# A post-norm transformer block: rotation and gating in PSUM, row maxima in pairs, a third bank for products

## The chip, the cores and the metric

The kernel runs on one core of a Trainium2 chip. A core has five engines that matter here: TensorE (matrix products; PE in the profile, PEld its weight loads), VectorE (DVE), ScalarE (ACT), GpSimd (POOL) and SyncE (SP), which here only issues transfers. They run beside each other; each works through its own instructions in order and waits on semaphores for the others. Matrix products land in PSUM, a small memory of eight banks, each holding 512 float32 numbers in each of 128 partitions. Operands and results otherwise lie in SBUF. The metric is the device time of one execution in microseconds; times are medians of several runs.

## What is computed

```python
def attn(x, Wq, bq, Wk, bk, Wv, bv, Wo, bo):        # 16 query heads of 32, one key/value head
    q = (x @ Wq + bq).reshape(B, T, H, HD).transpose(0, 2, 1, 3)
    k, v = (x @ Wk + bk)[:, None], (x @ Wv + bv)[:, None]
    q, k = rotary(q), rotary(k)      # [x1*cos - x2*sin, x2*cos + x1*sin] of the two halves of a head
    attn = softmax(q @ k^T / sqrt(HD))
    return (attn @ v).transpose(0, 2, 1, 3).reshape(B, T, D) @ Wo + bo

def ffn(x, w1, w2, w3):              # weights are made ternary: clip(round(w / mean|w|), -1, 1)
    return bitlinear(sigmoid(bitlinear(x, w1)) * bitlinear(x, w2), w3)

x = layernorm(x + attn(x, ...))
x = layernorm(x + ffn(x, ...))
```

B = 4 batches, T = 512 rows, D = 512, F = 1408 hidden columns; all float32.

## The kernel before

One core does all four batches in one program. Everything is laid out with features on the partitions: 512 features are NC = 4 chunks of 128 (a chunk is four heads), 512 rows are NT = 4 tiles of 128, the 1408 hidden columns are NF = 11 tiles.

**Order.** The program's order on every engine is written by hand: each helper (`act`, `dve`, `pool`, `mm`, `move`) pins its instruction to the place in which it is emitted, so the Python code from line 679 is the schedule. It walks 64 *steps*, one for each batch b, chunk c and tile t. A step emits, in this order: `scores` of this tile (lines 375 to 410: transposed scores of four heads into two double banks of `ps_sc`, minus the row maxima, then exponentials `es` on ScalarE); `weigh` of the step before (line 416, the product with v, into `acc`); row maxima for the step LEAD = 7 ahead (`find_maxima`, line 705); and *fill*. Fill is other work in pieces of about 1.8 us: projections of later batches (`project_in`, line 237), the output projection (`project_out`, line 517) and the feed-forward (`feed_forward`, line 551). `fill.draw(us)` (line 661) emits pieces until the drawn time is used up, with `least` at least one; the time that a step draws is `pace`, 1.8, 3.8, 4.8 and 4.6 us for the four batches. Work with a delay stands in the list `late`; `due()` (line 689), called twice in a step, counts a slot and advances what has come due: the spreading of maxima, `normalize`, loads of x, layer norms, stores of q.

**Two kinds of step.** Up to step PER + 4 = 20, maxima are found in pairs of tiles, both before the fill, and `quantize` (2 or 3 jobs a step, three in each of the seven lead steps) emits the ternary weights: an absolute sum over each raw weight tile, or a sign on ScalarE and a `scalar_tensor_tensor` on VectorE (tile `raw`), with loads and stores on POOL's queue. From step 20 on the maxima come as one tile, two tiles, one tile, with fill between them. A single one goes into the bank with the tag `den`, a pair into a double bank of `ps_sc` (line 348).

**Banks.** `ps_sc` has two double banks, `ps_acc` one bank `acc` and one bank `den`, `ps_mm` two banks `mm` for all other products.

**Rotation.** `turn` (line 225) is a generator in two halves. A projection lands in a bank; ScalarE copies it with its bias into SBUF (`r` or `kv`); the first half on VectorE makes a = (product + bias) * cos from PSUM, which together with the copy frees the bank. After the next piece of fill the second half swaps the halves of each head (`stream_shuffle` of the copy into `w`), multiplies `w` by the signed sine table in SBUF and adds a and w.

**Gating.** `feed_forward` makes tanh of the gate product on ScalarE (`th`), then hw = (th + 1) * up from PSUM into SBUF on VectorE, which frees the bank, and `split` (line 506) cuts hw into a rounded head (ScalarE) and a tail (VectorE) for two exact single-pass products.

**POOL.** From the second batch on POOL adds up the exponentials (`total`, four additions in a step), and normalizes: `normalize` (line 432) copies the row sums to SBUF, sends them through DRAM into a compact tile `few`, takes the reciprocal on VectorE, sends it back and spreads it (`rden`), and multiplies on POOL, one `due` turn for each stage. `load_x` (line 494) loads the four tiles of x and adds bo on POOL, all four in one turn.

Of the kernel before, what the change touches and what calls it, by code (L numbers as in the profile page):

```python
# [27 lines left out]
def postln_block(  # L28
# [74 lines left out]
    wo_sb = const.tile([P, NC, D], F32, name="wo_sb")  # L103
    bq_sb = const.tile([P, NC], F32, name="bq_sb")
    bkv_sb = const.tile([P, 1], F32, name="bkv_sb")
    bo_sb = const.tile([P, D], F32, name="bo_sb")
# [50 lines left out]
    def quantized():  # L157
# [38 lines left out]
        for k, (m, last, f) in enumerate(jobs):  # L196
# [18 lines left out]
            yield  # L215


    swap = [(i + HALF) % HD for i in range(HD)]
# [5 lines left out]

    def turn(outs, src, bias, r, n):

        w = work.tile([P, T], F32, tag="rot_b", name="w")
        a = work.tile([P, T], F32, tag="rot_c", name="a", bufs=1)
        dve.scalar_tensor_tensor(a[0:n], src[0:n], bias[0:n], cos_sb[0:n], ALU.add, ALU.mult)
        yield  # L230
        dve.stream_shuffle(w[0:n], r[0:n], swap)
        dve.tensor_tensor(w[0:n], w[0:n], sin_sb[0:n], ALU.mult)
        for out, rows in outs:
            dve.tensor_tensor(out, a[rows], w[rows], ALU.add)
        yield

    def project_in(b):

        s = batches[b]
        n = P - HD  # L240
        while now < NC * NT * (b - 2):
            yield 0

        pk = ps_mm.tile([P, T], F32, tag="mm", name="pk")
# [4 lines left out]
        kv = work.tile([P, T], F32, tag="rot_a", name="kv")  # L249
        act.activation(kv, pk, AF.Identity, bias=bkv_sb)  # L250
        s.kT = work.tile([P, T], F32, tag="kT", name="kT", bufs=3)
        rotation = turn(
            [(s.kT[0:n], slice(0, n)), (s.kT[n:P], slice(0, HD))], pk, bkv_sb, kv, n
        )
        next(rotation)
        yield 1.8
        next(rotation)
        if b > 0:
            late.append((slot + 2, split_k(b)))
        for c in range(NC):  # L260

            while b + 1 == B and c + 2 >= NC and not batches[0].projected:
                yield 0
            pq = ps_mm.tile([P, T], F32, tag="mm", name="pq")
            for d in range(NC):
                mm(pq, wq_sb[c][:, d, :], s.xT[d], d == 0, d == NC - 1)
                if d == 1:
                    yield -1.8
            r = work.tile([P, T], F32, tag="rot_a", name="r")
            act.activation(r, pq, AF.Identity, bias=bq_sb[:, c : c + 1])  # L270
            if b == 0:

                if c == 0:
                    room = work.tile([P, NC, T], F32, tag="y0", name="room", bufs=1)
                q = s.q[c] = room[:, c, :]
            else:
                q = work.tile([P, T], F32, tag="q", name="q")
            rotation = turn([(q, slice(0, P))], pq, bq_sb[:, c : c + 1], r, P)
            next(rotation)
            if c == 0:  # L280
                pv = ps_mm.tile([P, NT, HD], F32, tag="mm", name="pv")
# [4 lines left out]
            yield 1.8  # L286
            next(rotation)
            if b > 0:
                late.append((slot + 2, store_q(b, c, q)))
            s.done = c + 1  # L290
        load_xT(NC if b == 0 else 2)

# [49 lines left out]
    def maximum(b, c, i, chunks, q):  # L342


        s = batches[b]
        if i == 0 and chunks[0] == 0:
            s.mx[c] = small.tile([P, NG, NT], F32, tag="mx", name="mx")
        if len(chunks) == 1:
            ps = ps_acc.tile([P, 1, T], F32, tag="den", name="pmax")
        else:  # L350
            ps = ps_sc.tile([P, 2, T], F32, tag="sc", name="pmax")
        for n, t in enumerate(chunks):
            mm(ps[:, n, :], q[:, ts(t, P)], s.kr, True, True)
        dve.tensor_reduce(s.mx[c][:, i, chunks[0] : chunks[-1] + 1], ps, AX.X, ALU.max)

    def spread(b, c):


        s = batches[b]
        pm = ps_mm.tile([NG * NT, P], F32, tag="mm", name="pm")  # L360
# [12 lines left out]
        yield  # L373
# [58 lines left out]
    def normalize(b, c):  # L432

        s = batches[b]
        if b > 0:
            s.den = ps_acc.tile([P, T], F32, tag="den", name="den")
            columns(s.den, ones[:, 0:HD], s.total, True, True)

        sums = work.tile([P, T], F32, tag="sums", name="sums", bufs=1)
        act.copy(sums, s.den)  # L440
        yield
        flat = [dram.tile([NG, T], F32, tag=f"flat{i}", name="flat", bufs=3) for i in range(2)]
        move(flat[0], sums.rearrange("(i r) k -> i r k", r=HD)[:, 0])
        yield
        few = small.tile([P, NG * T // P], F32, tag="few", name="few")
        move(few, flat[0].rearrange("i (r j) -> (i r) j", r=HD))
        yield
        dve.reciprocal(few, few)
        move(flat[1].rearrange("i (r j) -> (i r) j", r=HD), few)
        yield  # L450
        rden = work.tile([P, T], F32, tag="rden", name="rden", bufs=1)
        for i in range(NG):
            move(rden[ts(i, HD), :], flat[1][i].partition_broadcast(HD))
        yield
        pool.tensor_tensor(s.ctxT[c], s.ctxT[c], rden, ALU.mult)
        yield
# [37 lines left out]
    def load_x(b):  # L494
        batches[b].x = []
        for t in range(NT):
            xt = xp.tile([P, D], F32, tag="x", name="xt")
            move(xt, x[b, ts(t, P), :])
            batches[b].x.append(xt)
        yield  # L500
        for xt in batches[b].x:
            pool.tensor_tensor(xt, xt, bo_sb, ALU.add)
        yield

# [12 lines left out]
    def project_out(b):  # L517
# [4 lines left out]
        for t in range(NT):  # L522
            po = ps_mm.tile([P, D], F32, tag="mm", name="po")
            for c in range(NC):
# [16 lines left out]
        for t in range(NT):  # L541
            pt = ps_mm.tile([P, NC, P], F32, tag="mm", name="pt")
            for c in range(NC):
# [7 lines left out]
    def feed_forward(b):  # L551
# [8 lines left out]
        def product(k, m):  # L560
# [3 lines left out]
            if len(w3[k]) < len(parts[k]):  # L564
                w3[k].append(load_weight(2, parts[k][len(w3[k])]))
            g = ps_mm.tile([P, T], F32, tag="mm", name="gu")
            for c in range(NC):
# [13 lines left out]
        for k, fs in enumerate(parts):  # L581
            h = []
            for f in fs:
# [3 lines left out]
                up = product(k, 1)  # L587
                hw = work.tile([P, T], F32, tag="hw", name="hw")
                dve.scalar_tensor_tensor(hw, th[f], 1.0, up, ALU.add, ALU.mult)
                s.y_done = f == NF - 1  # L590
                yield 1.9
                h.append([hp.tile([P, T], F32R, tag="h", name=f"h{i}") for i in range(2)])
                split(*h[-1], hw)
            if fs[-1] + 1 < NF:
                gate(k + 1, fs[-1] + 1)
                yield 1.9
            for t in range(NT):

                while fs[-1] + 1 == NF and b + 1 < B and 0 <= batches[b + 1].transposed <= t:
                    yield 0  # L600
                po = ps_mm.tile([P, D], F32, tag="mm", name="po")
                for n, w in enumerate(w3[k]):
# [143 lines left out]
    for n, (b, c, t) in enumerate(steps):  # L746
# [94 lines left out]
```

## Time and profile before

| | |
|---|---|
| median of 3 runs | 710.61 us (707.37 to 710.65) |
| the profiled execution's own time | 711.07 us |
| its span, first to last instruction | 709.2 us |
| mean granted TensorE clock | 0.978 |
| instructions | 9580 |

The profile is of one execution. "Busy" is the time in which an engine has at least one instruction under way. Groups of instructions are told by line, but here nearly all have the line of the pinning helper (L74, L79), so they are told apart by their tiles, out<-in. A group's line ends with the engine's idle time just before its instructions and what ended it. The clock row gives in tenths what share of TensorE's full clock was granted in each fortieth of the span. Some groups of the trace, in us:

| group | count | busy | mean ns |
|---|---|---|---|
| PE gu<-y,wg, gate and up products | 704 | 173.1 | 395 |
| PE po<-wd,h, third product of the feed-forward | 352 | 90.9 | 403 |
| PE pmax<-kr,qr, products for maxima from batch 2 on | 192 | 80.6 | 478 |
| DVE mx<-pmax, maxima of pairs (128x1024) | 91 | 108.7 | 1215 |
| DVE mx<-pmax, maxima of single tiles (128x512) | 74 | 50.6 | 683 |
| DVE hw<-th,gu, gating | 44 | 30.2 | 687 |
| ACT h<-hw, head of the split | 44 | 27.3 | 620 |
| ACT r<-pq, copies for the rotation | 16 | 10.9 | 684 |
| DVE a<-pq, cosine product | 16 | 11.9 | 745 |
| DVE w<-r, shuffle | 16 | 11.7 | 730 |
| POOL total<-total,es | 96 | 124.9 | 1333 |

### The profile page before, as it was taken

Reading aid. Unit: us, or ns where it says so; the run is one execution under the profiler, and the core shown is the slowest. Engines: PE = TensorE matmul, PEld = TensorE weight load, DVE = VectorE, ACT = ScalarE, POOL = GpSimd, SP = SyncE. Lnnn points to the kernel's source line nnn. Section 1 sums busy time; section 2 is a strip of 40 time slices with the busy share of each in tenths; the row PEclk is TensorE's granted clock in tenths of the full one; section 3 lists DMA queues with packets and bytes.
Section 4 is the critical chain, followed back from the end, with each engine's and each line's share of the span. In section 5 each row is a group of like instructions: output and inputs, shape, how many; then the busy total and the mean of one; then the engine's idle time right before and its main releaser. Section 6 shows DMA issues by size and latency. Waiting matters only on the chain.

```text
span 709.2 us, 9580 instructions
## 1 busy us (share of the span) xinstructions
PE 670.7 (95%) x3318; PEld 362.7 (51%) x3318; DVE 409.4 (58%) x577; ACT 297.2 (42%) x464; POOL 326.8 (46%) x412
## 2 busy tenths in 40 slices
PE   7989999979879989999999999999998999999994
PEld 5333333333324435556446565554454676768882
DVE  0897766868975564646554765455534333463334
ACT  1456657645423454424325445243434421224213
POOL 3224433545977566639374474667573812202000
PEclk9999999989979989999999999999999999999998
DMA  8663877689734147427214247351130464235531
GB/s 286 212 230 127 252 218 228 220 249 315 230 107 115 54 126 233 137 66 234 72 52 123 75 152 225 105 170 58 46 103 21 138 218 135 74 104 182 189 104 60
DMA packets 59663, 107.20 MB, mean 151 GB/s; under 512 B 13664, under 2 KB 14176, under 8 KB 59616
## 3 DMA queue, kind: packets, MB, share of 16 engines
q1 hardware_dynamic: 51696, 80.64, 36.5%
q0 software_dynamic: 7920, 25.96, 11.1%
q8 instruction: 26, 0.43, 0.2%
q14 instruction: 21, 0.17, 0.1%
HBM read 83.76 MB, written 22.81 MB: 150 GB/s over the span
## 4 chain that ended last, share of the span: by engine, by line
PE 77%; DVE 12%; DMA 2%; issue 2%; ACT 1%; SPq 1%; POOL 1%; DVEq 0%; ACTq 0%; POOLq 0%
PE gu L79 23%; PE po L79 19%; PE ps L79 11%; PE pmax L79 8%; PE acc L79 8%; PE pq L79 4%; PE den L79 3%; DVE mx L74 3%; DVE w L74 3%; DVE xt L74 1%; SPq L82 1%; DVE raw L74 1%; DMA few<-flat 1%; DMA rden<-flat 1%; PE pt L85 1%
## 5 line engine op out<-in xcount | busy, mean ns | idle before, releaser
L74 DVE TENSOR_REDUCE mx<-pmax 128x1 f32<-128x512 f32 (+1 forms) x165 | 159.1, 976 | 101.6 <-PE pmax L79 101.6
L74 ACT ACTIVATE es<-ps 128x1024 f32<-128x1024 f32 x128 | 124.1, 1021 | 132.6 <-PE ps L79 124.6
L79 PE MATMUL gu<-y,wg 128*128 128x512 f32 x704 | 173.1, 395 | 0.9 <-DVE xt L74 0.6
L79 PEld LDWEIGHTS gu<-y,wg 128*128 128x128 f32 x704 | 130.9, 188 | 39.8 <-issue 5.3
L74 POOL TENSOR_TENSOR total<-total,es 128x512 f32<-128x512 f32 x96 | 124.9, 1333 | 38.3 <-ACT es L74 38.1
L79 PE MATMUL po<-wd,h 128*128 128x512 f32 x352 | 90.9, 403 | 7.1 <-DVE xt L74 2.9
L74 POOL TENSOR_TENSOR total<-es 128x512 f32<-128x512 f32 x48 | 61.4, 1311 | 76.7 <-ACT es L74 76.7
L79 PE MATMUL pmax<-kr,qr 128*128 128x512 f32 x192 | 80.6, 478 | 3.2 <-DVE mx L74 2.4
L79 PEld LDWEIGHTS po<-wd,h 128*128 128x128 f32 x352 | 65.5, 190 | 30.3 <-DVE xt L74 5.3
L79 PE MATMUL acc<-es,v 128*32 128x512 f32 x512 | 70.8, 626 | 0.0
L79 PEld LDWEIGHTS pmax<-kr,qr 128*128 128x128 f32 x192 | 35.3, 192 | 60.0 <-issue 28.5
L74 DVE SCALAR_TENSOR_TENSOR hw<-th,gu 128x512 f32<-128x512 f32 x44 | 30.2, 687 | 57.5 <-PE gu L79 55.8
L74 DVE SCALAR_TENSOR_TENSOR xt<-po,xt 128x512 f32<-128x512 f32 x48 | 33.2, 691 | 51.8 <-PE po L79 51.7
L74 POOL DMA_DIRECT2D raw<-in_wf x66 | 35.8, 545 | 57.9 <-ACT junk L74 29.5
L74 ACT CAST h<-hw 128x512 fp32r<-128x512 f32 x44 | 27.3, 620 | 83.8 <-DVE hw L74 83.8
L79 PE MATMUL ps<-qT,kT 32*128 32x512 f32 x384 | 58.1, 660 | 4.2 <-DVE mx L74 4.2
L79 PE MATMUL po<-wo_sb,ctxT 128*128 128x512 f32 x128 | 61.4, 608 | 0.3 <-DVE hw L74 0.3
L79 PE MATMUL ps<-negm,ones_r 2*128 2x512 f32 x256 | 60.6, 810 | 0.0
L74 DVE TENSOR_TENSOR h<-hw,h 128x512 fp32r<-128x512 f32 x44 | 42.5, 965 | 26.4 <-ACT h L74 26.1
L79 PE MATMUL pq<-xT,wq_sb 128*128 128x512 f32 x112 | 53.6, 604 | 3.5 <-DVE m L74 1.5
L74 ACT ACTIVATE th<-gu 128x512 f32<-128x512 f32 x44 | 26.3, 597 | 46.2 <-PE gu L79 46.2
L79 PEld LDWEIGHTS po<-wo_sb,ctxT 128*128 128x128 f32 x128 | 24.3, 194 | 23.2 <-issue 20.8
(86 smaller groups left out, 646.9 us busy)
## 6 DMA issues: line engine op xcount, KB each, us to landing
wg<-w SPq DMA_DIRECT2D x88, 256.0 KB
raw<-in_wf POOLq DMA_DIRECT2D x66, 256.0 KB, 4.7
qr<-qp SPq DMA_DIRECT2D x96, 128.0 KB
wd<-w SPq DMA_DIRECT2D x44, 256.0 KB
w<-raw POOLq DMA_DIRECT2D x33, 256.0 KB, 4.8
qp<-q SPq DMA_DIRECT2D x48, 128.0 KB
rden<-flat SPq DMA_DIRECT2D x64, 64.0 KB
xt<-in_x SPq DMA_DIRECT2D x16, 256.0 KB
```

Of the source, the lines that this page charges most:

```text
L74: return lambda *args, **kw: pin(getattr(self.engine, name)(*args, **kw))
L79: pin(nc.tensor.matmul(out, lhsT=lhsT, rhs=rhs, start=start, stop=stop))
L82: pin(nc.sync.dma_start(out=out, in_=in_))
L85: pin(nc.tensor.transpose(out, in_, identity))
```

## The change

1. `turn` is no longer a generator. The shuffle works in place on the product's own bank in PSUM, without a copy; the bias that belongs to it is added afterwards, already swapped on the host (a second set of columns in `bq_sb` and `bkv_sb`). ScalarE's copies of q go; that of kv keeps the 32 rows of v. All four VectorE instructions are emitted together behind the product, and the bank is held until the last.
2. Row maxima come in pairs in every step, always into `ps_sc`.
3. `bank` gives every third of the other products the bank `den`, from step 20 on. Row sums of later batches are among these products.
4. (th + 1) * up is written back into its bank in PSUM, and the split reads it there.
5. The early kind of step lasts until the last batch's queries are projected. After it, a step draws 0.4 of its fill (at least one piece) before the two pairs of maxima and 0.6 after them. `quantize` makes 2 or 3 jobs a step (7 in three steps).
6. `normalize` waits one turn more before the reciprocal and one more before the product on POOL, but for the last chunk of a batch. `load_x` adds bo to one tile of x in a turn.

```diff
+    turns = iter(range(10**6))
+
+    def bank(shape, name):
+        if now >= PER + NT and next(turns) % 3 == 2:
+            return ps_acc.tile(shape, F32, tag="den", name=name)
+        return ps_mm.tile(shape, F32, tag="mm", name=name)
...
-    def turn(outs, src, bias, r, n):
-        w = work.tile([P, T], F32, tag="rot_b", name="w")
-        a = work.tile([P, T], F32, tag="rot_c", name="a", bufs=1)
-        dve.scalar_tensor_tensor(a[0:n], src[0:n], bias[0:n], cos_sb[0:n], ALU.add, ALU.mult)
-        yield
-        dve.stream_shuffle(w[0:n], r[0:n], swap)
-        dve.tensor_tensor(w[0:n], w[0:n], sin_sb[0:n], ALU.mult)
+    def turn(outs, ps, bias, turned, n):
+        a = work.tile([P, T], F32, tag="rot_c", name="a")
+        dve.scalar_tensor_tensor(a[0:n], ps[0:n], bias[0:n], cos_sb[0:n], ALU.add, ALU.mult)
+        dve.stream_shuffle(ps[0:n], ps[0:n], swap)
+        dve.scalar_tensor_tensor(ps[0:n], ps[0:n], turned[0:n], sin_sb[0:n], ALU.add, ALU.mult)
         for out, rows in outs:
-            dve.tensor_tensor(out, a[rows], w[rows], ALU.add)
-        yield
+            dve.tensor_tensor(out, a[rows], ps[rows], ALU.add)
...
-            pq = ps_mm.tile([P, T], F32, tag="mm", name="pq")
+            pq = bank([P, T], "pq")
...
-            r = work.tile([P, T], F32, tag="rot_a", name="r")
-            act.activation(r, pq, AF.Identity, bias=bq_sb[:, c : c + 1])
...
-        if len(chunks) == 1:
-            ps = ps_acc.tile([P, 1, T], F32, tag="den", name="pmax")
-        else:
-            ps = ps_sc.tile([P, 2, T], F32, tag="sc", name="pmax")
+        ps = ps_sc.tile([P, 2, T], F32, tag="sc", name="pmax")
...
         if b > 0:
-            s.den = ps_acc.tile([P, T], F32, tag="den", name="den")
+            s.den = bank([P, T], "den")
...
         move(few, flat[0].rearrange("i (r j) -> (i r) j", r=HD))
         yield
+        if c + 1 < NC:
+            yield
         dve.reciprocal(few, few)
...
         yield
+        if c + 1 < NC:
+            yield
         pool.tensor_tensor(s.ctxT[c], s.ctxT[c], rden, ALU.mult)
...
         for xt in batches[b].x:
             pool.tensor_tensor(xt, xt, bo_sb, ALU.add)
-        yield
+            yield
...
-                hw = work.tile([P, T], F32, tag="hw", name="hw")
-                dve.scalar_tensor_tensor(hw, th[f], 1.0, up, ALU.add, ALU.mult)
+                dve.scalar_tensor_tensor(up, th[f], 1.0, up, ALU.add, ALU.mult)
...
-                split(*h[-1], hw)
+                split(*h[-1], up)
...
-        if n < PER + 4:
+        if batches[-1].done < NC:
             find_maxima(n + LEAD, 0, 1)
             due()
             find_maxima(n + LEAD, 2, 3)
-            quantize(2)
+            quantize(1 if n % 3 else 2)
             fill.draw(pace)
-            quantize(n % 2)
+            quantize(1)
         else:
-            find_maxima(n + LEAD, 0)
-            fill.draw(0.4 * pace)
-            find_maxima(n + LEAD, 1, 2)
+            fill.draw(0.4 * pace, True)
+            find_maxima(n + LEAD, 0, 1)
+            find_maxima(n + LEAD, 2, 3)
             due()
-            fill.draw(0.3 * pace, True)
-            find_maxima(n + LEAD, 3)
-            fill.draw(0.3 * pace)
+            fill.draw(0.6 * pace)
         due()
```

`bank` takes the place of `ps_mm.tile` also for pk, pv, pm, both kinds of po, pt and gu.

More of the change, by code (lines that the diff above doesn't have):

```diff
@@ L103, in postln_block @@
     wo_sb = const.tile([P, NC, D], F32, name="wo_sb")
-    bq_sb = const.tile([P, NC], F32, name="bq_sb")
-    bkv_sb = const.tile([P, 1], F32, name="bkv_sb")
+    bq_sb = const.tile([P, 2 * NC], F32, name="bq_sb")
+    bkv_sb = const.tile([P, 2], F32, name="bkv_sb")
     bo_sb = const.tile([P, D], F32, name="bo_sb")
@@ L242, in project_in @@
             yield 0
-        pk = ps_mm.tile([P, T], F32, tag="mm", name="pk")
+        pk = bank([P, T], "pk")
         for c in range(NC):
@@ L248, in project_in @@
                 yield -1.8
-        kv = work.tile([P, T], F32, tag="rot_a", name="kv")
-        act.activation(kv, pk, AF.Identity, bias=bkv_sb)
+        kv = work.tile([P, T], F32, tag="kv", name="kv", bufs=1)
+        act.activation(kv[n:P], pk[n:P], AF.Identity, bias=bkv_sb[n:P, 0:1])
         s.kT = work.tile([P, T], F32, tag="kT", name="kT", bufs=3)
-        rotation = turn(
-            [(s.kT[0:n], slice(0, n)), (s.kT[n:P], slice(0, HD))], pk, bkv_sb, kv, n
+        turn(
+            [(s.kT[0:n], slice(0, n)), (s.kT[n:P], slice(0, HD))],
+            pk, bkv_sb[:, 0:1], bkv_sb[:, 1:2], n,
         )
-        next(rotation)
         yield 1.8
-        next(rotation)
         if b > 0:
@@ L277, in project_in @@
                 q = work.tile([P, T], F32, tag="q", name="q")
-            rotation = turn([(q, slice(0, P))], pq, bq_sb[:, c : c + 1], r, P)
-            next(rotation)
+            turn([(q, slice(0, P))], pq, bq_sb[:, c : c + 1], bq_sb[:, NC + c : NC + c + 1], P)
             if c == 0:
-                pv = ps_mm.tile([P, NT, HD], F32, tag="mm", name="pv")
+                pv = bank([P, NT, HD], "pv")
                 for t in range(NT):
@@ L285, in project_in @@
                 act.copy(s.v, pv)
-            yield 1.8
-            next(rotation)
             if b > 0:
@@ L290, in project_in @@
             s.done = c + 1
+            yield 1.8
         load_xT(NC if b == 0 else 2)
@@ L359, in spread @@
         s = batches[b]
-        pm = ps_mm.tile([NG * NT, P], F32, tag="mm", name="pm")
+        pm = bank([NG * NT, P], "pm")
         transpose(pm, s.mx[c].rearrange("p i t -> p (i t)"), ident)
@@ L522, in project_out @@
         for t in range(NT):
-            po = ps_mm.tile([P, D], F32, tag="mm", name="po")
+            po = bank([P, D], "po")
             for c in range(NC):
@@ L541, in project_out @@
         for t in range(NT):
-            pt = ps_mm.tile([P, NC, P], F32, tag="mm", name="pt")
+            pt = bank([P, NC, P], "pt")
             for c in range(NC):
@@ L565, in product @@
                 w3[k].append(load_weight(2, parts[k][len(w3[k])]))
-            g = ps_mm.tile([P, T], F32, tag="mm", name="gu")
+            g = bank([P, T], "gu")
             for c in range(NC):
@@ L600, in feed_forward @@
                     yield 0
-                po = ps_mm.tile([P, D], F32, tag="mm", name="po")
+                po = bank([P, D], "po")
                 for n, w in enumerate(w3[k]):
@@ L811, with swapped @@
     bk, bv = np.asarray(L0_attn_bk), np.asarray(L0_attn_bv)
+    bkv = np.concatenate([bk, bk, bk, bv])[:, None]
+    bq = np.asarray(L0_attn_bq).reshape(-1, P).T
+    def swapped(a):
+        return a.reshape(P // HD, 2, HALF, -1)[:, ::-1].reshape(a.shape)
     ins = {
@@ L815 @@
         "wq": np.asarray(L0_attn_Wq).reshape(NC, P, NC, P).transpose(1, 2, 0, 3),
-        "bq": np.asarray(L0_attn_bq).reshape(-1, P).T,
+        "bq": np.concatenate([bq, swapped(bq)], axis=1),
         "wkv": np.concatenate([wk, wk, wk, wv], axis=1).reshape(NC, P, P).transpose(1, 0, 2),
-        "bkv": np.concatenate([bk, bk, bk, bv])[:, None],
+        "bkv": np.concatenate([bkv, swapped(bkv)], axis=1),
         "wo": L0_attn_Wo,
```

## The prediction

> **What bounds the kernel now.** I read the page first, then the windows, then the timeline of the poorest windows, then the groups by shape.
>
> ```profile
> PE 670.7 (95%) x3318; PEld 362.7 (51%) x3318; DVE 409.4 (58%) x577; ACT 297.2 (42%) x464; POOL 326.8 (46%) x412
> PEclk9999999989979989999999999999999999999998
> ```
>
> TensorE is busy 95% of the span and no edit takes a matmul away. A gain can only come from its 709.2 - 670.7 = 38.5 us of idle time, and from the stretches in which its clock digit is below 9. The windows place them (columns: stretch, length, busy us of PE, PEld, DVE, ACT, POOL, granted clock, DMA share, GB/s):
>
> ```profile
> 144.80:154.80 10.00, 6.44 (x37) 2.61 (x36) 5.74 (x11) 5.18 (x7) 4.26 (x7) 1.00 0.75 239
> 154.80:165.00 10.20, 10.18 (x38) 3.38 (x38) 5.16 (x6) 3.15 (x4) 3.42 (x6) 0.67 0.91 272
> 191.00:201.10 10.10, 5.59 (x29) 2.03 (x28) 10.00 (x4) 3.03 (x4) 9.94 (x9) 0.94 0.68 220
> 201.10:214.00 12.90, 12.83 (x40) 4.61 (x40) 7.70 (x9) 3.75 (x6) 7.70 (x7) 0.65 0.26 75
> 214.00:221.00 7.00, 7.00 (x34) 2.88 (x33) 4.24 (x7) 2.21 (x3) 4.93 (x5) 1.00 0.65 182
> ```
>
> The last row is a sound step. Each stall is followed by a stretch at a granted clock near 0.66, so it is paid almost twice. The timeline says who stalls:
>
> ```profile
> 153.43 0.25 DVE L74 RECIPROCAL few<-few 128x16 f32<-128x16 f32 x1 [4.14 <-DMA few<-flat]
> ...
> 154.82 2.35 PE L79 MATMUL ps<-room,kT 32*128 32x512 f32 x6 [3.58 <-DVE mx L74]
> ...
> 187.91 4.94 POOL L74 TENSOR_TENSOR total<-total,es 128x512 f32<-128x512 f32 x4
> 190.78 7.53 DVE L74 TENSOR_TENSOR w<-w,sin_sb 128x512 f32<-128x512 f32 x1
> 192.82 4.93 POOL L74 TENSOR_TENSOR xt<-xt,bo_sb 128x512 f32<-128x512 f32 x4
> ...
> 201.17 2.35 PE L79 MATMUL ps<-qT,kT 32*128 32x512 f32 x6 [4.24 <-DVE mx L74]
> ...
> 253.97 1.57 DVE L74 TENSOR_TENSOR q<-a,w 128x512 f32<-128x512 f32 x1
> 256.17 0.67 DVE L74 TENSOR_TENSOR y<-pt,y 128x512 fp32r<-128x512 f32 x1
> ```
>
> Stall A: scores wait for maxima that queue on VectorE behind a reciprocal, which waits for a DMA. Stall B: one sine product stands 7.53 us while POOL runs eight additions without a pause. At 253.97, under POOL additions, the rotation's sum (two SBUF inputs) takes 1.57 us; at 256.17, also under POOL, y (one PSUM input) takes 0.67. By shape (busy us, mean ns):
>
> ```profile
> L74 DVE TENSOR_TENSOR h<-hw,h 128x512 fp32r<-128x512 f32 x44 | 42.5, 965 | 26.4 <-ACT h L74 26.1
> L74 DVE TENSOR_TENSOR w<-w,sin_sb 128x512 f32<-128x512 f32 x16 | 21.1, 1317 | 0.6
> L74 DVE TENSOR_TENSOR q<-a,w 128x512 f32<-128x512 f32 x12 | 11.9, 988 | 1.0
> L74 DVE TENSOR_TENSOR y<-pt,y 128x512 fp32r<-128x512 f32 x16 | 10.8, 673 | 1.2 <-ACT y L74 1.2
> ```
>
> **Gains, stall by stall.** Lost time is the step's length (from one step's first score to the next's) less that of a sound one.
>
> A (reciprocal one turn later): steps 144.77 to 154.82 and 154.82 to 164.98, against 6.4 (118.33 to 124.75), lost 3.6 + 3.8 = 7.4. A turn is about half a step, 3.3 us; the wait was 4.14, and the two reductions (2.3) now go ahead of it. I take 6.
>
> B: the four steps from 173.02 to 214.09 last 41.1. A sound step with two halves of a product takes 6.85 (221.06 to 227.91), so 3.4 without its two times 1.72. Four times 3.4, seven halves (12.0), a den (0.9), the v transposes (0.45) and three waits for the exponentials (0.6 each) make 28.8: lost 12. The rotation's three contended operations drop to PSUM prices, and POOL's bo additions come one per turn. But sign steps (raw, two SBUF inputs) remain there, slightly more of them, since quantizing 45 remaining jobs at 2.33 instead of 2.5 per step ends one step later; POOL's totals can hold them. I take 9.
>
> C (249.78 to 267.30, 17.5 us against two times 3.4 plus four pt at 0.55 and a gu of 1.84, 10.8): q and w contended, pt waiting for one of two banks, a maximum waiting for its only bank. Lost 6.7; four transposes with 0.67 us of VectorE each still meet two reductions. I take 4.
>
> D (ends of a feed-forward, po waiting for h): idle 1.05 at 399.18, 2.0 around 541.9 to 544.9, 1.5 of slow clock behind. h falls from 1.68 to 0.67 there: I take 2.5.
>
> E (two-bank waits elsewhere): po's 7.1 and gu's 0.9 idle, less D's 3.1 and the tail's 1.3, leave 3.6; a third bank: 2. The tail itself gives nothing: its chain is VectorE's 2.4 us per row block (xt at 695.70, 698.11, 700.52).
>
> Sum 23.5. Removed ScalarE copies (16 x 0.68 = 11 us) and some 25 us of VectorE (h 44 x 0.29, w 16 x 0.6, q 12 x 0.3) count only through these stalls: from 280 to 540 PE is at 19.7 to 20.0 of 20 in most windows. So does the joining of maxima itself: reductions of 0.68, 1.22 and 0.68 per step become two of 1.22, 0.15 us less.
>
> **Costs.** *Rotation in PSUM.* Now a 0.745, shuffle 0.730, product and sum 0.69 each uncontended = 2.86 us; new the same four. No row writes PSUM from VectorE: below, nothing gained over 0.69; above, twice, if read and write shared a way, 1.5 us more per rotation, which only the prologue (DVE 18.1 of 20) would show, about 9 us. I take equal, by y (PSUM read). The Trainium skill speaks against the edit: "VectorE: DVE Perf Modes", Rules for kernel authors, lets one copy PSUM to SBUF first where many operations follow, PSUM input running at the single rate. By that rule four operations on PSUM lose. The rows say no: sine products in SBUF never fall below 0.686 (y 0.673), so nothing is lost, and contention goes.
>
> In one piece, the rotation holds its bank and stands before the next maxima. Prologue: v's transposes wait for pk's bank to 20.0 instead of 19.0, the next product 0.7 to 2.9 behind; reductions shift but VectorE stays full: 1.3. First batch: two reductions 2.4, two sign steps 1.6, a rotation 2.9 are 6.9 us of VectorE in a 6.5 us step, every second step, and 4.0 in the other; the next reductions start some 0.4 late and a part reaches the scores: 1.5 in all.
>
> *Held up.* The bank is kept for 0.69 + ScalarE 0.62 + 0.67 plus hand-overs, 2.3 us, instead of 0.9. "PSUM — Partial Sum Buffer", Summary, says to evacuate promptly. With two banks, asked for again after one product (1.81), that would cost 0.5 x 44 = 22 us; with three, asked for after 3.6, nothing. All products of this kind come after step 20, so nothing; if the cover fails, those 22.
>
> *Order of a step.* Steps 20 to 26 keep the early order (until the last batch is projected, 249 us). There both maxima follow weigh at once and want the score banks. Step 182.32 shows it: pmax at 184.81 and 185.72 instead of 184.62 and 185.27, 0.64 lost: 7 x 0.6 = 4.2.
>
> From 27 on, one fill piece covers the exponentials. If it ends at E, VectorE has its evacuation until E+0.9 (STT 302.75 after pmax 302.55), reductions to E+2.0 and E+3.1. A single piece behind (0.9 + 1.8) brings the next scores at E+2.75, their second half at E+3.0: 0.2 lost. At 4.8 us of fill, every other step has one piece: 18 x 0.2 = 3.6. Bounds: 0 (reductions first) and 0.8 in all 37 steps (h ahead too).
>
> *Waits added.* normalize's two extra turns push rden and POOL's ctxT back one step; next user is project_out, which only the last chunk feeds, and that one skips them. Behind them on SP and POOL nothing else moves. load_x's last addition comes in feed's turn, 1.4 us of POOL before x is read. Nothing.
>
> Sum 1.3 + 1.5 + 4.2 + 3.6 = 10.6. Net 23.5 - 10.6 = 12.9 under the profiled execution's 711.07 (span plus 1.87): **698**; that execution is 0.46 above the median of the runs.
>
> **Rivals.** *Clean gain*: single pieces seldom fall and early-order waits vanish behind pieces; gains 27, costs 1: 685. For: sound steps have 3 us of idle VectorE in 7. Against: 182.32's waits are this order's.
>
> *Joined maxima become the wait* (slower): place, scores from step 20 on; price, both reductions plus whatever VectorE has before them; with h ahead 0.67 us per step, 44 x 0.67 = 29.5, so 711 - 23.5 + 2.8 + 29.5 = 720. It decides from (23.5 - 2.8) / 44 = 0.47 us per step. For: in-order VectorE, two score buffers. Against: 2.6 pieces in most steps.
>
> *The stalls only move* (the change doesn't do what it says): sign steps under POOL's additions, or a DMA later than a turn, restart the slow clock; A and B give 3 instead of 15, 711 - 11.5 + 10.6 = 710. For: seven of the sign steps fall under POOL's totals (from step 17), and 2.61 us went to one POOL split there. Against: the late turn alone nearly covers A.
>
> **How the numbers follow.** Forecast 0.48 (own range 688 to 708), clean 0.18, joined wait 0.25, moved 0.09. About 0.5% (3.6 us) is what a measurement can tell: faster 0.65, same 0.09, slower 0.26. The range goes from the clean case to the joined wait, leaving out their far ends: 682 to 719.
>
> **What would show it.** Right: no sine product above 0.8 us, h near 0.67, no PE stall over 2 us at 150 and 190, fewer clock digits below 9, PE busy again about 95% of a shorter span. Wrong: ps waiting on mx in many steps after 270 (joined wait), gu waiting on h (bank hold), rotation operations over 0.8 us (PSUM price), a half-speed stretch in the prologue.

## The result and the profile after

The changed kernel takes 715.99 us (median of 7, 712.84 to 717.45) against 710.51 (707.37 to 712.24) for the kernel before beside it: ratio 1.0067, interval 1.0039 to 1.0095. It is slower by 0.4 to 1.0%, where 698 was forecast. Its profiled execution took 716.06 us, span 714.3 (before 709.2), mean clock 0.976 (0.978). Two rows of the page after, busy time by engine and the clock by fortieths:

```profile
PE 675.6 (95%) x3318; PEld 365.8 (51%) x3318; DVE 383.3 (54%) x540; ACT 285.3 (40%) x448; POOL 315.3 (44%) x412
PEclk9998999999879999999999999999999999999998
```

The other engines did shed work: VectorE 409.4 to 383.3, ScalarE 297.2 to 285.3, POOL 326.8 to 315.3. TensorE's idle time stayed, 714.3 - 675.6 = 38.7 us against 38.5, and so did the stretches at half clock ahead of the tail, 27.3 us in both, at other places. The stalls were exchanged, not removed. The 5.1 us that the span grew stand as busy time of the same 3318 matmuls; part of it is waiting all the same, since a row of products that follows POOL step by step counts as busy here (`den` below: 5.32 us instead of 1.06). The first two windows of before (columns as in the prediction):

```profile
20.00:40.00 20.00, 18.52 (x63) 6.37 (x65) 18.10 (x25) 7.99 (x23) 5.32 (x10) 1.00 0.60 202
40.00:60.00 20.00, 18.74 (x94) 6.74 (x86) 16.25 (x22) 14.36 (x37) 8.15 (x14) 1.00 0.57 188
```

The same two after, and three more:

```profile
20.00:40.00 20.00, 17.21 (x54) 5.95 (x56) 15.68 (x23) 5.90 (x19) 5.33 (x10) 0.91 0.64 226
40.00:60.00 20.00, 15.69 (x59) 5.30 (x57) 15.73 (x21) 9.07 (x28) 3.72 (x7) 0.97 0.40 122
153.84:161.02 7.18, 7.12 (x37) 2.64 (x36) 4.53 (x7) 3.25 (x5) 3.11 (x5) 1.00 1.03 352
183.51:197.87 14.36, 9.89 (x37) 3.70 (x36) 14.24 (x16) 4.66 (x7) 11.99 (x12) 0.79 0.41 122
204.08:220.16 16.08, 12.99 (x41) 3.50 (x40) 5.27 (x7) 3.52 (x5) 12.30 (x10) 0.79 0.32 103
```

The third of these rows is one of the two steps of stall A, 10.05 us before and 7.18 now. The last two are stall B, still there: in the first of them VectorE is busy 14.24 of 14.36 us, POOL 11.99, TensorE only 9.89. New is the loss in the first two: from 40 to 60 TensorE was busy 18.74 us before, now 15.69, and VectorE isn't full either. Where the time went, by the start of steps (the first score of each, from the timeline; change against before, in us; predicted are the prediction's terms, the 0.6 of each early-order step put where it falls):

| stretch | predicted | measured |
|---|---|---|
| start to step 1 (lead steps and prologue) | +1.3 | +9.6 |
| steps 1 to 13 | +1.5 | +0.4 |
| 13 to 16, stall A | -6 | -7.5 |
| 16 to 22, stall B and two early-order steps | -7.8 | +4.2 |
| 22 to 26, early order | +2.4 | +2.3 |
| 26 to 29, stall C | -3.4 | -4.9 |
| 29 to 61, new order and third bank | +1.6 | +4.6 |
| 61 to 62, stall D | -2.5 | -3.1 |
| rest | 0 | -0.5 |
| sum | -12.9 | +5.1 |

Six rows are as predicted within 1.5 us. Three are not: the prologue was priced 8.3 too low, B 12.0, and 29 to 61 3.0, where one step, 57, alone is 3.5 longer than before. (Here and below "step 57" as a length is the time up to the first score of step 57.) Together that is 23.3; the six others give 5.3 back. The timeline of before in the prologue (a bracket is the engine's idle time before the line, and what ended it):

```profile
25.20 2.35 DVE L74 TENSOR_REDUCE mx<-pmax 128x2 f32<-128x1024 f32 x2
26.64 2.09 PE L79 MATMUL pmax<-kT,room 32*128 32x512 f32 x8
27.47 0.72 DVE L74 STREAM_SHUFFLE w<-r 128x512 f32<-128x512 f32 x1
```

The timeline after, at the three places:

```profile
24.82 0.75 DVE L74 SCALAR_TENSOR_TENSOR a<-pq,bq_sb,cos_sb 128x512 f32<-128x512 f32 x1 [1.72 <-PE pq L79]
...
27.62 4.81 DVE L74 TENSOR_REDUCE mx<-pmax 128x2 f32<-128x1024 f32 x4
28.89 2.26 PE L79 MATMUL pmax<-kT,room 32*128 32x512 f32 x8 [1.13 <-DVE mx L74]
...
34.59 0.75 DVE L74 SCALAR_TENSOR_TENSOR a<-pq,bq_sb,cos_sb 128x512 f32<-128x512 f32 x1 [2.16 <-PE pq L79]
...
180.92 4.94 POOL L74 TENSOR_TENSOR total<-es 128x512 f32<-128x512 f32 x4
...
182.13 6.46 DVE L74 SCALAR_TENSOR_TENSOR raw<-raw,hi,sgn 128x512 f32<-128x512 f32 x1
...
192.14 0.63 PE L85 MATMUL pv<-ident,kv 32*128 32x32 f32 x4 [2.77 <-DVE kT L74]
...
207.03 0.50 PE L79 MATMUL ps<-negm,ones_r 2*128 2x512 f32 x4 [1.79 <-DMA negm<-rows]
...
210.82 5.32 PE L79 MATMUL den<-total,ones 128*32 128x512 f32 x8 [1.17 <-POOL total L74]
...
505.29 0.69 DVE L74 SCALAR_TENSOR_TENSOR gu<-th,gu 128x512 f32<-128x512 f32 x1
...
513.96 0.68 DVE L74 TENSOR_TENSOR h<-gu,h 128x512 fp32r<-128x512 f32 x1
514.70 2.59 PE L79 MATMUL gu<-y,wg 128*128 128x512 f32 x8 [2.69 <-DVE h L74]
```

**Prologue.** Before, the reductions stood ahead of the shuffle, and TensorE's next maxima started at 26.64 without a wait. After, VectorE runs a whole rotation from 24.82, and only at 27.62 the reductions that have waited since TensorE finished the maxima. TensorE, in order, stands 1.13 us before its next maxima until a score bank is free; the next product comes late by that, and at 34.59 VectorE waits 2.16 for it. Each waits for the other in turn.

**B.** A sign step (two SBUF inputs) lasts 6.46 us while POOL adds; alone it takes 0.74. Behind it in order stands k's rotation, which now holds its bank until its last sum, and at 192.14 v's transposes have waited 2.77 for that bank. Step 21, the last row of the windows, has waits of another kind: one of the row maxima's transfers (`negm`) comes 1.79 us late, and then the eight products of the row sums (`den`) follow POOL's four additions one by one, for 5.32 us, partly at half clock.

**Step 57.** The gated value lies in its bank from 505.98; its split ends only at 514.64, and TensorE has waited 2.69 for the bank.

By shape (busy us, mean ns), the costs that no row of before could show:

```profile
L74 DVE TENSOR_TENSOR h<-gu,h 128x512 fp32r<-128x512 f32 x44 | 30.1, 685 | 35.8 <-ACT h L74 35.6
L74 DVE SCALAR_TENSOR_TENSOR pq<-pq,bq_sb,sin_sb 128x512 f32<-128x512 f32 x16 | 12.1, 759 | 0.6
L74 DVE STREAM_SHUFFLE pq<-pq 128x512 f32<-128x512 f32 x16 | 11.1, 693 | 0.0
L74 DVE TENSOR_TENSOR q<-a,pq 128x512 f32<-128x512 f32 x12 | 8.3, 688 | 0.9
```

Reading and writing the same PSUM bank costs next to nothing extra (0.69 and 0.76 us), and no rotation operation is stretched by POOL any more (the sine product was 1.317 in the mean, q's sum 0.988). The edit did to its operations what it should. Its order did the harm.

### The profile page after: what moved, and what is told of

The parts are those of the page before. It is cut to its first block, busy times and chain, and to the rows that moved or that the text cites. A ratio compares the mean times of both kernels' runs of the same rounds, so it can differ in the third digit from the quotient of the medians.

```text
span 714.3 us, 9500 instructions
## 1 busy us (share of the span) xinstructions
PE 675.6 (95%) x3318; PEld 365.8 (51%) x3318; DVE 383.3 (54%) x540; ACT 285.3 (40%) x448; POOL 315.3 (44%) x412
## 5 line engine op out<-in xcount | busy, mean ns | idle before, releaser
L74 DVE TENSOR_REDUCE mx<-pmax 128x2 f32<-128x1024 f32 x128 | 151.2, 1215 | 70.8 <-PE pmax L79 70.5
L79 PEld LDWEIGHTS gu<-y,wg 128*128 128x128 f32 x704 | 130.4, 188 | 52.2 <-issue 12.9
L74 POOL TENSOR_TENSOR total<-total,es 128x512 f32<-128x512 f32 x96 | 120.4, 1286 | 44.8 <-ACT es L74 44.7
L74 POOL TENSOR_TENSOR total<-es 128x512 f32<-128x512 f32 x48 | 60.0, 1281 | 82.6 <-ACT es L74 82.6
L74 DVE SCALAR_TENSOR_TENSOR gu<-th,gu 128x512 f32<-128x512 f32 x44 | 30.6, 695 | 81.5 <-PE gu L79 64.8
L79 PE MATMUL acc<-es,v 128*32 128x512 f32 x512 | 68.2, 605 | 0.0
L79 PE MATMUL ps<-negm,ones_r 2*128 2x512 f32 x256 | 63.6, 789 | 1.8 <-DMA negm<-rows 1.8
L79 PE MATMUL ps<-qT,kT 32*128 32x512 f32 x384 | 62.2, 654 | 0.3 <-DVE mx L74 0.3
L79 PE MATMUL pmax<-kr,qr 128*128 128x512 f32 x192 | 59.6, 424 | 2.5 <-ACT es L74 2.0
L74 ACT CAST h<-gu 128x512 fp32r<-128x512 f32 x44 | 25.9, 590 | 88.4 <-DVE gu L74 88.4
L79 PE MATMUL pq<-xT,wq_sb 128*128 128x512 f32 x112 | 56.4, 634 | 3.3 <-ACT v L74 1.8
L74 DVE TENSOR_TENSOR h<-gu,h 128x512 fp32r<-128x512 f32 x44 | 30.1, 685 | 35.8 <-ACT h L74 35.6
L79 PEld LDWEIGHTS po<-wo_sb,ctxT 128*128 128x128 f32 x128 | 23.5, 189 | 28.8 <-issue 26.6
```

Of the source, the lines that this page charges most:

```text
L74: return lambda *args, **kw: pin(getattr(self.engine, name)(*args, **kw))
L79: pin(nc.tensor.matmul(out, lhsT=lhsT, rhs=rhs, start=start, stop=stop))
```

## The experiments

No kernel here leaves anything out. There are three groups of runs (e1 to e4; e5 to e8; e9, e10 and c3), each with its own runs of the kernel before, so ratios are compared, not medians. The stretches are from one profile each, in us; where two kernels have the same program up to a place, as e6 and e10 up to the feed-forward, they show how far single profiles differ, up to some 2 us in a stretch.

| kernel | ratio (interval) | step 1 at | 1 to 13 | 13 to 16 | 16 to 22 | 22 to 63 | 63 to end |
|---|---|---|---|---|---|---|---|
| before | 1 | 56.8 | 80.8 | 27.3 | 56.1 | 335.6 | 152.5 |
| after | 1.0067 (1.0039 to 1.0095) | 66.5 | 81.2 | 19.9 | 60.2 | 334.3 | 152.3 |
| e4_rotation_alone | 1.0029 (1.0007 to 1.0051) | 66.2 | 84.4 | 19.8 | 55.9 | 333.2 | 152.4 |
| e1_halves | 0.9970 (0.9939 to 1.0002) | 59.2 | 82.6 | 19.9 | 56.8 | 334.4 | 152.3 |
| e2_early_quant | 1.0105 (1.0058 to 1.0151) | 69.4 | 85.2 | 25.6 | 49.4 | 334.7 | 152.3 |
| e3_both | 0.9947 (0.9927 to 0.9968) | 59.0 | 87.5 | 22.1 | 49.5 | 334.4 | 152.3 |
| e5_no_extension | 1.0115 (1.0071 to 1.0158) | 66.4 | 81.2 | 19.8 | 55.9 | 339.2 | 152.3 |
| e6_lead_halves | 0.9915 (0.9881 to 0.9949) | 57.3 | 82.4 | 23.5 | 50.8 | 334.4 | 152.3 |
| e7_gate_sbuf | 1.0073 (1.0035 to 1.0111) | 68.5 | 81.2 | 19.8 | 59.6 | 332.8 | 151.5 |
| e8_turns_alone | 0.9915 (0.9887 to 0.9942) | 57.3 | 81.0 | 19.5 | 54.3 | 334.1 | 152.8 |
| e9_two_banks | 1.0400 (1.0337 to 1.0462) | 65.1 | 81.1 | 19.8 | 62.4 | 340.6 | 166.5 |
| e10_split_at_once | 0.9964 (0.9934 to 0.9994) | 57.4 | 82.4 | 25.7 | 48.8 | 341.0 | 151.3 |
| c3_few_edits | 0.9845 (0.9807 to 0.9882) | 60.2 | 83.3 | 21.7 | 49.1 | 330.9 | 152.4 |

### The rotation in one piece: e4 and e1

e4 puts the new `turn` alone into the kernel before (one line of the edit):

```diff
-            rotation = turn([(q, slice(0, P))], pq, bq_sb[:, c : c + 1], r, P)
+            turn([(q, slice(0, P))], pq, bq_sb[:, c : c + 1], bq_sb[:, NC + c : NC + c + 1], P)
```

> The kernel before with the PSUM rotation in one piece and nothing else of the change. Theory L: the prologue loses as in the changed kernel, step 0 near 56 and step 1 near 65; stall A at 150 stays; the stall at 190 is shorter or longer by which of rotation and sign steps meets POOL's totals; 711 to 718 in all. Rival (the prologue's loss comes from the other edits, such as the order of turns): step 0 near 51.

Step 1 starts at 66.2, 9.3 us late: the whole loss of the prologue is the rotation's. e4 also has no stall A (19.8 us from 13 to 16), though it lacks the extra turns: with its steps some 13 us later there, none of its reciprocals there waits for a transfer. It gets new stalls at step 10 (10.63 us) and at step 17 (14.69 us), where TensorE waits 3.21 us for the transfer of `negm`.

e1 takes the changed kernel and cuts the rotation in two again, still in PSUM (the lines that resume it are left out):

```diff
         dve.scalar_tensor_tensor(a[0:n], ps[0:n], bias[0:n], cos_sb[0:n], ALU.add, ALU.mult)
+        yield
         dve.stream_shuffle(ps[0:n], ps[0:n], swap)
...
```

> The changed kernel, with its PSUM rotation cut in two again: after the cosine product the generator yields, and shuffle, sine product and sum come one piece of fill later. Theory L (lockstep: the whole rotation ahead of the reductions makes TensorE and VectorE wait for each other in the prologue): step 0 starts near 51 us instead of 56.9 and step 1 near 58 instead of 66.5, the half-speed stretches at 31 and 59 us go, and the time falls by 7 to 9 us. Rival H (the held bank costs it: v's transposes and later products wait for the rotation's bank): halves hold the bank longer still, so step 0 stays at 56 or later. Rival P (operations that write PSUM are slow): no change, since the same operations run.

Step 1 comes at 59.2, 7.3 us earlier than after, with the same instructions and the same tiles. Not the price of PSUM but the order on VectorE costs the time. The stall of B moved one step ahead: a sign step of 7.06 us under POOL's first additions, in a step of 14.84 us. So halves alone do not cure B.

### Sign steps ahead of POOL's additions: e2, e3, e6

POOL's `total` additions begin with step 17. e2 makes three quantizing jobs a step, so that the last sign step falls in step 14; e3 joins it with e1.

```diff
-            quantize(1 if n % 3 else 2)
+            quantize(2)
             fill.draw(pace)
```

> The changed kernel with three quantizing jobs in every step, so that the last sign step is out in step 14, before POOL's totals begin in step 17. Theory S (a sign step with two SBUF inputs, shut out by POOL's totals for 6.46 us at 182.13, holds up k's rotation, with it v's transposes, and all that follows): no sign step over 1.5 us, steps 18 to 22 take about 35 us instead of 44, the half-speed stretches at 192 and 209 us go, and the time falls by 7 to 10 us. Rival Y (the added turns of normalize and load_x make POOL and SP late): den still waits for total and negm for its DMA near 205 to 215, steps 18 to 22 stay at 42 or more. Both: up to 2 us may be lost in steps 0 to 14 to a fuller VectorE.

> Both edits: rotation in two halves and three jobs a step. Theories L and S together: the gains add up, 715 - 8 - 8 = 699 to 701, under the kernel before. If one stall merely moves to the next wait, less than half of the sum: 706 or more.

From 16 to 22 the two take 49.4 and 49.5 us instead of 60.2: most of B's stall is the sign steps under POOL's additions. What stays is step 21, 12.2 and 12.3 us, in which `den` still follows POOL's additions; the wait for `negm` and the half clock there are gone. But more jobs in earlier steps cost e2 4.0 us in steps 1 to 13 and 5.8 from 13 to 16, where ScalarE, in order, holds a sign back for its weights' transfer (up to 2.27 us) with the exponentials behind it. So e2 as a whole isn't faster. e3 takes 705.14 us, short of the 699 to 701 of the sum: it gains by the prologue, and loses 6.3 us in steps 1 to 13, most at step 10 (11.54 us), where TensorE waits 3.29 for the bank of a k that is held between its halves.

e6 uses halves in the lead only, one piece after, and 8 jobs in three steps (the lines that resume the rotation are again left out):

```diff
+        if now < 0:
+            yield
         dve.stream_shuffle(ps[0:n], ps[0:n], swap)
...
-            quantize(1 if n % 3 else 2)
+            quantize(2 if n % 3 else 1)
```

> The changed kernel with the rotation in halves only ahead of step 0, in one piece after, and 2.67 quantizing jobs a step instead of 2.33, so that the last sign step is out in step 16, before POOL's totals. Theories L and S: step 1 near 59 instead of 66.5 as with halves throughout, no stall near step 10 (there the halves held k's bank), no sign step over 2.5 us, steps 18 to 22 near 35 us: 698 to 701. Rival (faster quantizing starves on its weight DMAs and holds ScalarE, as three jobs a step did in step 15): 704 or more.

Ratio 0.9915, 702.98 us where 698 to 701 was expected: the same program with two edits of order is faster than before. Step 1 is at 57.3, and 16 to 22 takes 50.8. The timeline of e6 at the place that stalled after:

```profile
25.59 2.36 DVE L74 TENSOR_REDUCE mx<-pmax 128x2 f32<-128x1024 f32 x2 [0.32 <-PE pmax L79]
...
27.40 1.73 PE L79 MATMUL pmax<-kT,room 32*128 32x512 f32 x8
```

The reductions now stand ahead of the shuffle (which starts at 27.87), and TensorE's next maxima start with no wait. It pays 3.6 us from 13 to 16, and not for e2's reason. Stall A is back there:

```profile
154.22 0.25 DVE L74 RECIPROCAL few<-few 128x16 f32<-128x16 f32 x1 [2.34 <-DMA few<-flat]
155.61 0.70 PE L79 MATMUL ps<-room,kT 32*128 32x512 f32 x2 [1.75 <-DVE mx L74]
```

In spite of the added turn the reciprocal waits 2.34 us for its transfer (3.00 in e10), the scores 1.75 for the reduction behind it, and a half-clock stretch of 3.4 us follows at 156.9. In e8, below, with the same turns, the same reciprocal does not wait. What made the transfer late in e6 was not followed.

### The longer early order: e5

```diff
-        if batches[-1].done < NC:
+        if n < PER + 4:
```

> The changed kernel with one edit: the early kind of step ends at step 20 again, instead of when the last batch is projected (about step 26). Theory X (without a piece of fill ahead of the maxima they wait for the exponentials, 0.72 us a step in steps 22 to 24): those steps take 6.85 instead of 7.55 us, 4 to 5 us less in all, 711 to 712. Rival: the late order brings its own wait there (maxima behind fill, scores behind the reductions), no gain.

Steps 22 to 24 get shorter (6.85, 7.18 and 7.17 against 7.55 to 7.57), by 0.5 us in the mean, near the 0.6 of the prediction, but steps 26 and 27 take 8.46 and 9.09 instead of 5.84 and 6.19. The ratio isn't below after's: the longer early order is not a net cost. Its 0.6 us a step and the larger part of stall C's gain are one trade: 26 to 29 takes 24.4 us in e5, 21.5 after, 26.4 before.

### The held bank: e7, e9, e10

e7 puts the gated value back into SBUF (tile `hw`), e9 takes away the third bank, e10 (on e6) splits right behind the gating:

```diff
-                dve.scalar_tensor_tensor(up, th[f], 1.0, up, ALU.add, ALU.mult)
+                hw = work.tile([P, T], F32, tag="hw", name="hw")
+                dve.scalar_tensor_tensor(hw, th[f], 1.0, up, ALU.add, ALU.mult)
...
-                split(*h[-1], up)
+                split(*h[-1], hw)
```

> The changed kernel with the gated value written to SBUF again (hw), which frees its bank at once. Theory G (the held bank costs: in step 56 a gate product waits 2.7 us for the split, and the clock drops behind it): step 56 to 57 takes 8.2 us instead of 11.6, but the split's tail, now with two SBUF inputs, meets POOL again (mean above 0.9 us instead of 0.685) and steps 61 to 62 take 10 instead of 7.4: about 715, no change in sum. Rival (the wait comes from the order of urgent and other fill): step 56 still 11.6.

Step 57 falls from 11.64 to 8.51, which shows its cause. The tail h goes from 0.685 to 0.913 us in the mean, and steps 62 and 44 lose 1.0 and 0.6. By the profile's stretch 22 to 63 e7 is 1.4 better than after; the ratios (1.0073 and 1.0067) don't tell them apart. Gating in PSUM as such neither gains nor costs anything that shows.

```diff
-        if now >= PER + NT and next(turns) % 3 == 2:
+        if now >= PER + NT and next(turns) < 0:
```

> The changed kernel without the third bank: all products share the two banks. What the prediction claimed: a held up product then costs about 0.5 us each, 22 us in all, 730 to 740. Rival (the split comes out in time in most cases, only those put off by other fill wait): 5 us or less, 716 to 721.

The span is 735.5, 21.2 more than after (by the ratios some 24), where the prediction's failed cover was priced at 22. Two thirds of it (14.2) fall behind step 63, where little but the feed-forward is left and 22 of the 44 gated products are made: 0.65 us each. The other 22, between steps 22 and 63, cost 6.3 in sum, 0.3 each. The timeline of e9 behind step 63:

```profile
662.01 0.70 DVE L74 SCALAR_TENSOR_TENSOR gu<-th,gu 128x512 f32<-128x512 f32 x1 [2.20 <-PE gu L79]
...
662.74 0.59 ACT L74 CAST h<-gu 128x512 fp32r<-128x512 f32 x1 [1.96 <-DVE gu L74]
...
663.36 0.69 DVE L74 TENSOR_TENSOR h<-gu,h 128x512 fp32r<-128x512 f32 x1 [0.65 <-ACT h L74]
...
664.11 3.92 PE L79 MATMUL gu<-y,wg 128*128 128x512 f32 x16 [0.39 <-DVE h L74]
```

Gating, head and tail follow without a pause, 2.0 us in all, and the next gate product still waits 0.39 us for the bank. In such a row a gating comes every 4.30 us, 3.63 after.

```diff
                 s.y_done = f == NF - 1
-                yield 1.9
                 h.append([hp.tile([P, T], F32R, tag="h", name=f"h{i}") for i in range(2)])
                 split(*h[-1], up)
+                yield 1.9
```

> The lead-halves kernel with the split emitted directly behind the gating, ahead of the generator's turn, so that the bank is not held over other fill. Theory G (the bank is held because the split waits for the generator's next turn, which pieces of the output projection put off): step 56 takes 8.5 us instead of 12.1 and step 44 8.7 instead of 10.3, 4 to 5 us less than the 703 of that kernel. Rival (VectorE then waits in order for ScalarE's head, and the reductions behind it come late): scores wait on maxima from step 28 on, no gain or a loss.

Against e6, the expected gain comes: step 57 falls from 11.05 to 8.51 and step 62 from 7.36 to 6.14, but the stretch 22 to 63 is 6.6 us longer. The rival was right. The timeline of e10:

```profile
282.01 0.69 DVE L74 TENSOR_TENSOR h<-gu,h 128x512 fp32r<-128x512 f32 x1 [0.65 <-ACT h L74]
282.62 2.35 DVE L74 TENSOR_REDUCE mx<-pmax 128x2 f32<-128x1024 f32 x2
...
283.89 1.83 PE L79 MATMUL ps<-qT,kT 32*128 32x512 f32 x6 [0.60 <-DVE mx L74]
```

VectorE, in order, stands 0.65 us for ScalarE's head, the two reductions come behind that, and the next scores wait 0.60 for them, as they do in 16 places between 22 and 63 (4.0 us in sum); two stretches at half clock, 3.4 us each, begin at 286.6 and 296.8. Steps 31 to 33 take 8.86, 10.45 and 12.97 instead of 7.45, 7.49 and 10.70. That is the place of the rival "joined maxima become the wait", met once the split stands ahead of them.

### What most of the gain is: e8 and c3

e8 puts only edit 6, the extra turns, into the kernel before:

```diff
+        if c + 1 < NC:
+            yield
         dve.reciprocal(few, few)
...
             pool.tensor_tensor(xt, xt, bo_sb, ALU.add)
-        yield
+            yield
```

> The kernel before with the added turns alone (normalize waits one turn more at two places, load_x adds bo to one tile a turn). Theory A (the reciprocal waiting for its DMA held the reductions): steps 14 and 15 take 13 to 14 us instead of 20.2, and the time falls by 6 to 7 us, unless the stall at 190 grows. Rival (stall A went in the changed kernel because everything came 9 us later): steps 14 and 15 still 18 or more.

Ratio 0.9915, some 6 us, with a few lines. 13 to 16 takes 19.5 us instead of 27.3, and the reciprocal of stall A does not wait. Its step 18 still takes 13.51 us: q's sum, two SBUF inputs, lasts 4.15 us under POOL's additions. This is what the rotation in PSUM is for. c3 is the kernel before with the turns, the PSUM rotation (halves in the lead, one piece after) and the jobs of e6; banks, gating and step kinds stay as before. Two places of its edit, beside the new `turn` and the added turns:

```diff
         dve.scalar_tensor_tensor(a[0:n], ps[0:n], bias[0:n], cos_sb[0:n], ALU.add, ALU.mult)
+        if now < 0:
+            yield
         dve.stream_shuffle(ps[0:n], ps[0:n], swap)
...
-            quantize(n % 2)
+            quantize(1 if n % 3 else 0)
```

> The kernel before with three things alone: the added turns, the PSUM rotation (in halves ahead of step 0, in one piece after) and the last sign step out in step 16 (2.67 jobs a step). Banks, gating and both kinds of step stay. Theories L, S and A together, from the parts measured: the turns alone gave 9 us; no sign step above 2.5 us under POOL's totals gives some 5 more (step 18, 13.5 us with the turns alone, goes to 8.5), the rotation's contention at 250 to 259 some 3: 692 to 697. Rival (those gains need the third bank and the joined maxima): 700 or more.

697.88 us (696.49 to 699.6), ratio 0.9845: just above the expected range, the fastest of all, and faster than the changed kernel. From 16 to 22 it needs 49.1 against e8's 54.3, and from 22 to 63 it has the best figure of the table, 330.9, without third bank or PSUM gating.

## Why the prediction was wrong

**The prologue, predicted +1.3, measured +9.6.** The step that failed is "reductions shift but VectorE stays full". It counted VectorE's work, which the change doesn't raise, and took a busy engine (18.1 of 20 us from 20 to 40 before) for one that never waits. After, it is busy 15.68 of the same 20: four operations ahead of the reductions delay TensorE's maxima, TensorE's order delays the next product, and VectorE has nothing to do. e4 shows the cost with the rotation alone; with the order changed back e6 has 0.5 us of it left and e1 2.4. Some 4.3 of the 9.6 are TensorE's longer idle time up to step 1 (11.6 us, before 7.3). The rest is about what the clock takes: two stretches at half clock, 3.4 us from 31.4 and 6.8 from 58.7, cost up to 5, since half of such a stretch is lost. Their length agrees with the Trainium skill, "TensorE: Matmul & The Clock Gate", The HAM clock gate, by which the clock is decided over windows of about 3.4 us: after, all such stretches ahead of the tail were 3.4 or 6.8 us long. The prediction had named "a half-speed stretch in the prologue" as a sign of being wrong, and priced none.

**Stall B, predicted a gain of 9 (7.8 with its early-order steps), measured a loss of 4.2.** The failed term is "I take 9". The prediction took the stretched rotation operations for the stall's price, named the sign steps as what might remain, and left their price inside the 3 us that it didn't take. They did remain: one operation with two SBUF inputs in that stretch is enough, as 6.46 us after, 7.06 in e1 and 4.15 in e8 show. The one-piece rotation behind it then made v's transposes wait. All five kernels whose sign steps end before the additions begin and whose rotation is in PSUM take 48.8 to 50.8 us from 16 to 22 (e2, e3, e6, e10, c3), all eight others 54.3 to 62.4, though in e4 the long step is the one that waits for `negm`. So the rival "the stalls only move" was right for B. For A it was wrong in the changed kernel, but its "a DMA later than a turn" came true in e6 and e10.

**Held bank, predicted 0, measured 3.5 at one step.** The hold of 2.3 us was about right where the split follows at once (2.0 in e9). The failed step is "with three, asked for after 3.6, nothing": it left out a split that is put off. At step 57 output projections come between, and the bank stays held for 8.7 us (505.98 to 514.64); e7 gives 3.1 of the 3.5 back. The prediction had named the sign, "gu waiting on h". With two banks the 22 was right as a sum, 21.2, but not as 0.5 for each product: 0.65 behind step 63, 0.3 ahead of it. "PSUM — Partial Sum Buffer", Summary, asks for prompt evacuation: here it costs some 21 us to break that rule with two banks, and one stall with three.

**Right.** A: -6 forecast, -7.5 measured, and -7.9 in e8 alone. Luck may have helped in the changed kernel: the later steps alone took the stall away in e4, and in e6, without them, the added turn did not suffice. C: -3.4 and -4.9, of which some 3 belong to the longer early order, by e5; the prediction had that as a cost only. D: -2.5 and -3.1; of it about 1.0 belongs to the gating in PSUM, by e7, and 0.7 to the third bank, by e9. Early order: 2.4 and 2.3. New order from 29 to 61, but for step 57: 1.6 and 1.1. PSUM operations at equal price: 0.69 forecast, 0.69 and 0.76 measured. The rival of joined maxima (720) lies near the measured time by accident: without e10's edit no such wait runs through the steps after 270.

**Open.** The profile of one program's prologue varies: the five kernels that share after's lead order have step 1 at 65.1 to 69.4; those with halves, 57.3 to 60.2. Why stall A is absent in e4 and back in e6 isn't settled: no run follows that transfer. c3 has halves in the lead and still starts step 1 at 60.2. Its trace has a half-clock stretch of 6.8 us from 55.2, behind a wait of 1.11 us for the exponentials; before has the same wait (1.10) and no such stretch behind it. So some 3 us there differ from one profile to the next.

## What to carry to other kernels

When several operations are joined into one piece, ask first what stood between them in the engine's order: a busy engine that alternates with another has no slack to be moved into, though its work stays the same. A contended stretch is cured only when the last contended operation has left it, so count all of them before taking a gain. A transfer that is covered in one order of the program can be late in another. Try the edits of a large change apart: here a few added turns alone gave 0.85%, the whole change lost 0.67%, and a choice of its edits gave 1.55%.

## What the runs showed of the hardware

- An operation with two SBUF inputs on VectorE was sometimes held up by one POOL instruction and sometimes by a whole row of them. The sign step (0.74 us alone) took 6.46 after and 7.06 in e1, in each against four additions and a product of POOL, some 1.25 us each, that ran on without a pause. But in most cases, as at 253.97 before, the operation took 1.5 to 1.8 us, and POOL gave way: the four additions around it took 5.84 us instead of 4.94. "SBUF — State Buffer", Who interferes with whom, has whichever starts second wait until the first instruction is finished; that fits the short cases. What makes the long ones, no run here shows.
- Shuffle and product in place in PSUM, read and written by VectorE, took 0.693 and 0.759 us, no more than the shuffle in SBUF (0.730) and little more than a sine product in SBUF that nothing disturbed (0.686).
- In e10 the scores' waits of 0.53 and 0.60 us for the reductions, at 275.03 and 283.89, preceded the half-clock stretch at 286.6; no idle time there was longer in one piece. How much of e10's loss is the clock's wasn't measured apart.
